# Unread TensorE products, early ACT table loads and moved weight products in a four-stage image network on one core

## The chip, the core and the metric

The kernel runs on one core of one Trainium2 chip. The core has a matrix engine (TensorE, called PE in the profile, with its weight loads listed apart as PEld), three engines for elementwise work (VectorE or DVE, ScalarE or ACT, GpSimd or POOL) and SyncE (SP), which here only starts transfers. In the kernel each engine has its own list of instructions, and the lists wait for one another by semaphores. Matrix products are written to tiles in PSUM; all other tiles are in SBUF.

The metric is the device time of one execution in microseconds. A kernel's time is the median of its runs.

## What is computed

The input x is one image of 256 by 256 positions with 32 channels, in 32-bit floats. Four layers follow one another, and each has the form "x plus something of the group norm of x":

```python
x = x + _L0_conv_ref(_gn(x), ...)   # layer norm over channels, gates and values, projection
x = x + _L1_conv_ref(_gn(x))        # 3x3 mean, Sobel gradients, their magnitude
x = x + _L2_conv_ref(_gn(x))        # the same again
x = x + _L3_conv_ref(_gn(x), ...)   # two-layer gated recurrence over 256 steps
```

`_gn` normalises over all positions and pairs of channels, so no layer can begin before the layer ahead has ended: the mean and the variance need the whole image. In layer 0 the sequence axis has length one, so its softmax is 1 and what remains is sigmoid(n Wg) * (n Wv), then a product with Wo. The recurrence has 256 sequences, two layers and 128 hidden units; each step makes four gates per layer from a product, normalises each gate's 128 values, and updates a cell and a hidden state.

## The kernel before

Everything is kept in two SBUF tiles, `xa` and `xb`, of 128 partitions (4 columns of the image by 32 channels) by 64 blocks by 256 rows. Blocks are taken in 32 pairs of 512 columns, and most instructions are 128x512. Where the code is written inside `tc.manual_schedule()`, the engines' orders are the orders of the code; elsewhere a scheduler may move instructions.

The stages, in order:

- **Input** (lines 163 to 185). `nat` is loaded in 16 transfers, PE transposes it (L176), ACT copies it to `xa` (L183), DVE takes `bn_stats` (L184). `group_norm` (L136 to L156) then turns the statistics into `scale` and `bias`: DVE `mv` (L139), PE `pm` (L141), DVE `mean`, `d`, `q` (L143 to L147), PE `pv` (L149), ACT `std` by a square root (L151), DVE `scale` and `bias` (L153, L155). The same function serves all four layers, so there are four such seams.
- **LayerNorm** (L201 to L264). PE centres each pair (`pc`, L238), ACT squares it, DVE keeps it in `xb`, PE sums the squares into `pvar` (L228). Then ACT takes the root `std` (L248), DVE its reciprocal `rstd` (L249), PE spreads it over the channels (`pb`, L254), DVE multiplies (L261) and POOL applies gamma and beta (L262). Two small constant tiles for this stage, `avg` and `spread`, are made by POOL (L205 to L211) in a pool that opens after the input stage.
- **Attention** (L268 to L332): products `pg` and `pv` (L279), a sigmoid on ACT (`sg`, L294), a multiply on DVE (`o`, L297), the projection (L303), `r` on ACT (L311), an add on POOL (L313), `bn_stats` (L316).
- **Two Sobel layers** (`sobel_layer`, L345 to L504). For each pair k, ACT normalises (`xp`, `xn`, L376), DVE makes `u`, part of `pp`, `v` (L383, L392, L397), POOL the differences `dh` and sums `sh` (L405, L401), PE the products `centre` (L412, L422) and `edges` (L452) into two PSUM tiles `pg0` and `pg1` of three buffers each, ACT squares (L458), DVE adds (`ss`, L462), ACT takes the root in place in `pg1` (L466), DVE adds the residual (L469) and takes statistics (L472). The order on all engines is a written list: each part has a due time within a period of `every = 4.0`, and the list is sorted by it. The first Sobel layer also runs, after each pair's statistics, one entry of the list `between`: the centring of the recurrence's weights (`centring`, L583).
- **Recurrence weights.** `products` (L607 to L626) runs between the two Sobel layers, in the seam of the third group norm: a transpose `pl`, ACT's copy `latt`, POOL's repeats `lat4` and `wout4`, two products `pf` added to `bc` by DVE, a product `pe` copied into `e4` by four ACT copies and completed by POOL. `finish` (L628 to L655) runs after the fourth group norm: `sb` from scale and bias, two products `pg` copied to `fx` by ACT (L642), `pk` (L644, L645), `cst4`.
- **Recurrence** (`recurrence`, L720 to L906): four units (layer l, half h of the sequences) per step, interleaved by the due times of `PLAN` with a period of 8.7; `project` (L763) starts a unit's `zz` from the input `xt`, L790 and L795 add the hidden states' products, `sq`, `ve`, `rs` normalise, ACT makes gates, DVE and POOL the cell, PE transposes `h` into `pt` (L853). Outputs of block `blk` end in `st` (L883) and four transfers on SP's queue (L885). `sums` and `roots` hold 64 steps of small results (`SLOTS`).

ACT's functions come from tables: a root and a sigmoid need different ones, and a load (ACT_TABLE_LOAD) stands ahead of the first function that needs the other.

Of the kernel before, what the change touches and what calls it, by code (L numbers as in the profile page):

```python
# [10 lines left out]
F32 = mybir.dt.float32  # L11
AF = mybir.ActivationFunctionType
ALU = mybir.AluOpType
# [45 lines left out]
def net_kernel(  # L59
# [71 lines left out]
    NST = NB // 2  # L131

# [3 lines left out]
    def group_norm(stats, psum):  # L136

        mv = small.tile([P, nc.vector.BN_AGGR_DIM], F32, name="mv")
        nc.vector.bn_aggr(mv, stats)  # L139
        pm = psum.tile([P, 1], F32, name="pm", tag="pm", bufs=1)  # L140
        nc.tensor.matmul(pm, lhsT=kt[:, K_GN, :], rhs=mv[:, 0:1], start=True, stop=True)  # L141
        mean = small.tile([P, 1], F32, name="mean")
# [6 lines left out]
        nc.tensor.matmul(pv, lhsT=kt[:, K_GN, :], rhs=q, start=True, stop=True)  # L149
        std = small.tile([P, 1], F32, name="std")  # L150
# [5 lines left out]
        return scale, bias  # L156

# [5 lines left out]
    with tc.tile_pool(name="nat", bufs=3) as natp, tc.tile_pool(  # L163
# [21 lines left out]
        gn = group_norm(stats, ps_in)  # L185
# [9 lines left out]
    KS = NST // 4  # L195
# [5 lines left out]
    with tc.tile_pool(name="ln", bufs=4) as lnp:  # L201


        avg = lnp.tile([P, KS, KS, J], F32, name="avg", bufs=1)
        nc.gpsimd.memset(avg, 0.0)  # L205
        for ks in range(KS):
            nc.gpsimd.tensor_copy(avg[:, ks, ks, :], kt[:, K_AVG, 0:P:C])
        spread = lnp.tile([P, KS * J, C], F32, name="spread", bufs=1)
        for g in range(4):
            rows = slice(g * C, (g + 1) * C)  # L210
            nc.gpsimd.tensor_copy(  # L211
                spread[rows], ident[rows, rows].unsqueeze(2).to_broadcast([C, KS * J, C])
            )
        rstd = lnp.tile([P, 2 * S], F32, name="rstd", bufs=1)
        with tc.tile_pool(name="ps_ln", bufs=6, space=PSUM) as ps_ln, tc.tile_pool(
# [32 lines left out]
            nc.scalar.activation(std, pvar, AF.Sqrt, bias=ln_eps)  # L248
            nc.vector.reciprocal(rstd, std)  # L249
        with tc.tile_pool(name="ps_sp", bufs=8, space=PSUM) as ps_sp:  # L250
            for k, g, ks in pairs:
# [10 lines left out]
                nc.gpsimd.tensor_scalar(  # L262
                    pair(xb, k), pair(xb, k), gamma4, beta4, ALU.mult, ALU.add
# [5 lines left out]
    with tc.tile_pool(name="at", bufs=3) as atp, tc.tile_pool(  # L269
# [48 lines left out]
        with tc.manual_schedule():  # L318
            together((), [(0, j) for j in range(J)])
            together((), [(1, j) for j in range(2)])  # L320
            for i in range(NST):
# [5 lines left out]
                if i >= 1:  # L327
                    project(i - 1)
            for i in range(NST - 1, NST):
                project(i)  # L330
# [4 lines left out]
    with tc.tile_pool(name="ps_gn", bufs=1, space=PSUM) as ps_gn:  # L335
        gn = group_norm(stats, ps_gn)
# [8 lines left out]
    def sobel_layer(src, dst, scale, bias, between):  # L345
# [152 lines left out]
        with tc.manual_schedule():  # L498
            for _, k, part, args in todo:
                part(k, *args)  # L500
                if part is statistics and between:
                    between.pop(0)()
# [4 lines left out]
    with tc.tile_pool(name="ps_n", bufs=1, space=PSUM) as ps_n:  # L507
        gn = group_norm(stats, ps_n)
        rw.products(ps_n)
    stats = sobel_layer(xb, xa, *gn, [])  # L510
# [8 lines left out]
    with tc.tile_pool(name="ps_n", bufs=1, space=PSUM) as ps_n:  # L519
        gn = group_norm(stats, ps_n)  # L520
        weights = rw.finish(lw, ps_n, gn)
    with tc.If(plain > 0) as arms:
# [28 lines left out]
class RecurrentWeights:  # L551
# [31 lines left out]
    def centring(self):  # L583
# [21 lines left out]
        return [lambda p=out[i : i + 2]: [f() for f in p] for i in range(0, len(out), 2)]  # L605

    def products(self, psum):  # L607
        nc = self.nc
        pl = psum.tile([P, KX], F32, name="pl")
        nc.tensor.transpose(pl, self.lat, self.ident[:KX, :KX])  # L610
        nc.scalar.copy(self.latt, pl)
        for dst, src in ((self.lat4, self.latt[:, 0:C]), (self.wout4, self.wout)):
            nc.gpsimd.tensor_copy(dst, src.unsqueeze(1).to_broadcast([P, J, C]))
        for l in range(L):
            pf = psum.tile([KX, G], F32, name="pf", bufs=2)
# [3 lines left out]
        pe = psum.tile([P, C], F32, name="pe")  # L619
        nc.tensor.matmul(  # L620
            pe, lhsT=self.lat4.rearrange("p j c -> p (j c)"), rhs=self.wout, start=True, stop=True
        )
        for j in range(J):
            rows = slice(j * C, (j + 1) * C)
# [323 lines left out]
```

## Time and profile before

| | us |
|---|---|
| runs of before | 2879.49, 2883.52, 2886.28 (median 2883.52) |
| the profiled execution | 2880.13 |
| its span, first to last instruction | 2878.2 |
| PE busy in the span | 2776.8 (96%) |
| DVE, ACT, POOL busy | 2401.1, 2369.6, 1722.2 |
| input, from 0 to the end of the last `bn_stats` | 34.2 |
| LayerNorm, from the first `pc` to the first `pg` | 41.0 to 105.7 |
| attention, to the last `bn_stats` | 105.7 to 329.2 |
| first Sobel layer, first `xp` to last `bn_stats` | 334.3 to 479.2 |
| second Sobel layer | 485.1 to 627.1 |
| recurrence, from the first `zz` | 636.3 to 2878.2 |

The profile is of one execution. Its page gives busy shares per engine, the span in 40 slices of 72 us, the chain of work that ended last, and groups of instructions by line. Queries of the trace give the same for any stretch: a timeline (start, duration, engine, line, operation, tile written and tiles read, and in brackets the engine's idle time before and who ended it), the chain in order of time, and windows (each engine's busy time and the granted clock of PE in each). The granted clock is 1.00 or 0.50 in the windows of this trace that hold no change of it. A wait for several semaphores is put down to the one that came last by the profile.

### The profile page before, as it was taken

What the parts mean: (1) busy time and instruction counts of PE and PEld (TensorE: products, weight loads), DVE (VectorE), ACT (ScalarE), POOL (GpSimd) and SP (SyncE); (2) the same over time, 40 slices, a digit from 0 to 9 for tenths busy, and PEclk for the clock granted to TensorE, in tenths of its full rate; (3) what the DMA queues carried; (4) which work ended last, traced back from release to release, by engine and by line L of the source; (5) the groups of instructions that cost most, each with busy time, mean ns of one, the idle gap of its engine ahead of it and who ended that gap; (6) DMA issues with size and microseconds to landing.
All of it is one profiled execution on the core that took longest, in us unless ns stands there. A gap on an engine that the chain in (4) does not pass through costs nothing.

```text
span 2878.2 us, 38258 instructions
## 1 busy us (share of the span) xinstructions
PE 2776.8 (96%) x9561; PEld 1034.1 (36%) x9561; DVE 2401.1 (83%) x6505; ACT 2369.6 (82%) x6961; POOL 1722.2 (60%) x2076
## 2 busy tenths in 40 slices
PE   7899898989999999999999999999999999999997
PEld 4433333333333333333333333333333333333332
DVE  6788797977888888888888888888888888888886
ACT  5477676758888888888888888888888888888886
POOL 2311374656666666666666666666666666666665
PEclk9899998989999999999999999999999999999999
DMA  3000000000000000000000000000000000000000
GB/s 133 1 1 1 16 1 1 1 22 8 12 12 12 13 13 12 12 12 11 12 12 12 12 12 12 12 13 15 12 14 13 13 12 12 13 12 12 5 4 9
DMA packets 94333, 38.37 MB, mean 13 GB/s; under 512 B 74852, under 2 KB 91269, under 8 KB 94104
## 3 DMA queue, kind: packets, MB, share of 16 engines
q1 hardware_dynamic: 93156, 34.67, 5.1%
q8 instruction: 81, 1.33, 0.2%
q14 instruction: 148, 1.21, 0.1%
q10 hardware_dynamic: 148, 0.86, 0.1%
q0 software_dynamic: 800, 0.30, 0.0%
HBM read 10.63 MB, written 8.39 MB: 7 GB/s over the span
## 4 chain that ended last, share of the span: by engine, by line
PE 76%; DVE 9%; POOL 7%; ACT 5%; issue 1%; DVEq 0%; POOLq 0%; ACTq 0%
PE zz L795 26%; PE zz L770 15%; PE zz L790 11%; PE pt L853 5%; POOL rs L811 4%; PE pv L279 4%; PE pg L452 4%; DVE c L841 4%; PE pg L412 3%; DVE ve L808 3%; ACT sq L803 3%; PE pg L303 2%; POOL fc L837 2%; ACT ga L784 1%; PE px L871 1%; PE pg L279 1%
## 5 line engine op out<-in xcount | busy, mean ns | idle before, releaser
L811 POOL TENSOR_TENSOR rs<-ve,mhalf 128x4 f32<-128x4 f32 x1024 | 1040.6, 1016 | 539.6 <-DVE ve L808 539.5
L795 PE MATMUL zz<-wc,hT 128*128 128x512 f32 x2040 | 1102.3, 622 | 0.0
L784 ACT ACTIVATE ga<-zz,rs 128x128 f32<-128x128 f32 x3072 | 986.5, 368 | 29.1 <-POOL rs L811 9.9
L808 DVE TENSOR_REDUCE ve<-sq 128x4 f32<-128x516 f32 x1024 | 703.0, 687 | 52.1 <-ACT sq L803 37.2
L803 ACT ACTIVATE sq<-zz 128x512 f32<-128x512 f32 x1024 | 610.2, 596 | 150.9 <-PE zz L795 142.7
L770 PE MATMUL zz<-fx,xt 33*128 33x512 f32 x2048 | 591.7, 643 | 0.8 <-ACT fx L642 0.8
L790 PE MATMUL zz<-wc,hT 128*128 128x512 f32 x1024 | 524.5, 594 | 0.0
L795 PEld LDWEIGHTS zz<-wc,hT 128*128 128x128 f32 x2040 | 324.5, 188 | 555.6 <-DVE hT L857 399.0
L832 DVE TENSOR_TENSOR c<-ga 128x128 f32<-128x128 f32 x1024 | 299.4, 292 | 167.4 <-ACT ga L784 72.3
L845 ACT ACTIVATE th<-c 128x128 f32<-128x128 f32 x1024 | 316.0, 309 | 100.8 <-DVE c L841 100.7
L848 DVE TENSOR_TENSOR h<-go,th 128x128 f32<-128x128 f32 x1024 | 309.5, 302 | 96.9 <-ACT th L845 96.9
L784 ACT ACTIVATE go<-zz,rs 128x128 f32<-128x128 f32 x1024 | 378.8, 370 | 0.0
L837 POOL TENSOR_TENSOR fc<-ga,c 128x128 f32<-128x128 f32 x510 | 232.2, 455 | 244.0 <-ACT ga L784 244.0
L841 DVE TENSOR_TENSOR c<-c,fc 128x128 f32<-128x128 f32 x1020 | 361.6, 355 | 18.4 <-DVE hT L857 0.5
L853 PEld LDWEIGHTS pt<-ident,h 128*128 128x128 f32 x1024 | 142.8, 139 | 542.8 <-DVE h L848 542.3
L853 PE MATMUL pt<-ident,h 128*128 128x128 f32 x1024 | 294.3, 287 | 36.3 <-DVE h L848 36.2
L857 DVE COPY hT<-pt 128x128 f32<-128x128 f32 x1024 | 293.2, 286 | 10.2 <-PE pt L853 2.7
L770 PEld LDWEIGHTS zz<-fx,xt 33*128 33x128 f32 x2048 | 162.2, 185 | 260.6 <-ACT ga L784 193.2
L862 POOL TENSOR_TENSOR hs<-hT,hT 128x256 f32<-128x256 f32 x256 | 198.1, 774 | 2.5 <-DVE hT L857 2.5
L297 DVE TENSOR_TENSOR o<-pv,sg 128x512 f32<-128x512 f32 x256 | 158.1, 681 | 45.8 <-PE pg L279 37.7
L790 PEld LDWEIGHTS zz<-wc,hT 128*128 128x128 f32 x1024 | 162.4, 198 | 68.2 <-issue 56.4
L294 ACT ACTIVATE sg<-pg 128x512 f32<-128x512 f32 x256 | 138.6, 599 | 31.0 <-PE pg L279 25.0
(140 smaller groups left out, 2313.4 us busy)
## 6 DMA issues: line engine op xcount, KB each, us to landing
xt<-xa SPq DMA_DIRECT2D x256, 64.0 KB, 2.0
nat<-in_x_dram SPq DMA_DIRECT2D x16, 512.0 KB, 6.7
out_dram<-st SPq DMA_DIRECT2D x256, 32.0 KB, 1.7
wc<-in_L_conv_W_cell_dram SPq DMA_DIRECT2D x2, 512.0 KB, 4.6
kt<-in_consts_dram ACTq DMA_DIRECT2D x1, 832.0 KB, 5.8
wv<-in_L_conv_Wv_dram POOLq DMA_DIRECT2D x4, 32.0 KB, 4.1
wg<-in_L_conv_Wg_dram POOLq DMA_DIRECT2D x4, 32.0 KB, 5.5
gamma<-in_L_conv_ln_gamma_dram POOLq DMA_DIRECT2D x4, 0.1 KB, 5.9
```

The costliest lines, as they stand in the source:

```text
L770: nc.tensor.matmul(zz, lhsT=x, rhs=fx[rows, l, :], start=True, stop=l == 0 and t == 0)
L784: nc.scalar.activation(dst, gates(x, g), func, scale=scale)
L790: nc.tensor.matmul(get("zz"), lhsT=v["hT", 0, t][:, seqs], rhs=wc[:, l, 0, :], start=False, stop=t == 0)
L795: nc.tensor.matmul(get("zz"), lhsT=v["hT", l, t - 1][:, seqs], rhs=wc[:, l, 1, :], start=False, stop=True,)
L803: nc.scalar.activation(sqs[l, h][:, :, 0:H], four(get("zz")), AF.Square, scale=float(H**-0.5))
L808: nc.vector.tensor_reduce(ve, sqs[l, h], AX.X, ALU.add)
L811: nc.gpsimd.tensor_tensor(rs, get("ve"), inputs.mhalf, ALU.pow)
L832: nc.vector.tensor_mul(c, gates(get("ga"), 0), gates(get("ga"), 3))
L841: nc.vector.tensor_add(c, c, get("fc"))
L845: nc.scalar.activation(th, get("c"), AF.Tanh)
L848: nc.vector.tensor_mul(hh, get("go"), get("th"))
L853: nc.tensor.transpose(pt[:, 0:P], get("h"), ident)
```

## The change

Five things are changed.

1. `busy(psum, n, rhs)` issues n products of the identity with 256 columns into a PSUM tile `junk` that nothing reads. `group_norm` calls it before `pm` (3, 7, 3 and 3 products in the four seams), between `pm` and `pv` (2) and after `pv` (2, 12, 12 and 3). Nine more such products go into `pvar` after `std` of the LayerNorm, four follow the last `pb`, and the recurrence has six after its first two `zz` products and two after the next one.
2. `table(func, after)` issues a one-column activation that nothing reads. With Sqrt it follows the last input copy, and stands before the last projection's `r` of attention; with Sigmoid it follows the LayerNorm's `std`, and the fourth group norm's `scale`. The load of that table goes with it.
3. `avg` and `spread` are made at the start of the kernel in the constants' pool. Of the gamma/beta operations, every second one is ACT's instead of POOL's. `SLOTS` is 32 instead of 64.
4. `products` no longer runs between the Sobel layers. It returns five pieces that run after the statistics of pairs 0 to 4 of the second Sobel layer, with their PSUM tiles from the three buffers of `pg1`. In `finish`, the second `fx` copy is DVE's. The memsets of ones in `xt` are written after `finish`; in POOL's order they keep their place.
5. Of the last block's four output transfers, two are issued by ACT.

```diff
+    def table(func, after):
+        t = small.tile([P, 1], F32, name="table")
+        nc.scalar.activation(t, after, func, scale=0.0, bias=one)
+
+    def busy(psum, n, rhs=None):
+        junk = psum.tile([P, S], F32, name="junk", tag="junk", bufs=1)
+        for _ in range(n):
+            nc.tensor.matmul(
+                junk, lhsT=ident, rhs=kt[:, 0:2, :] if rhs is None else rhs, start=True, stop=True
+            )
...
-    def group_norm(stats, psum):
+    def group_norm(stats, psum, before, after, rhs=None):
...
         nc.vector.bn_aggr(mv, stats)
+        busy(psum, before, rhs)
         pm = psum.tile([P, 1], F32, name="pm", tag="pm", bufs=1)
         nc.tensor.matmul(pm, lhsT=kt[:, K_GN, :], rhs=mv[:, 0:1], start=True, stop=True)
+        busy(psum, 2, rhs)
...
         nc.tensor.matmul(pv, lhsT=kt[:, K_GN, :], rhs=q, start=True, stop=True)
+        busy(psum, after, rhs)
         std = small.tile([P, 1], F32, name="std")
...
-        gn = group_norm(stats, ps_in)
+        table(AF.Sqrt, xa[:, NB - 1, 0:1])
+        gn = group_norm(stats, ps_in, 3, 2, xa[:, NB - 1, :])
...
             nc.scalar.activation(std, pvar, AF.Sqrt, bias=ln_eps)
+            table(AF.Sigmoid, std[:, 0:1])
             nc.vector.reciprocal(rstd, std)
+            for _ in range(9):
+                nc.tensor.matmul(
+                    pvar[:, 0:S], lhsT=ident, rhs=kt[:, 0:2, :], start=True, stop=True
+                )
...
                 nc.vector.tensor_mul(pair(xb, k), pair(xb, k), pb)
-                nc.gpsimd.tensor_scalar(
-                    pair(xb, k), pair(xb, k), gamma4, beta4, ALU.mult, ALU.add
-                )
+                if i % 2:
+                    nc.scalar.activation(
+                        pair(xb, k), pair(xb, k), AF.Identity, scale=gamma4, bias=beta4
+                    )
+                else:
+                    nc.gpsimd.tensor_scalar(
+                        pair(xb, k), pair(xb, k), gamma4, beta4, ALU.mult, ALU.add
+                    )
+            junk = ps_sp.tile([P, 2 * S], F32, name="pb")
+            for _ in range(4):
+                nc.tensor.matmul(
+                    junk[:, 0:S], lhsT=ident, rhs=kt[:, 0:2, :], start=True, stop=True
+                )
...
+            table(AF.Sqrt, one)
             for i in range(NST - 1, NST):
                 project(i)
...
-        gn = group_norm(stats, ps_gn)
+        gn = group_norm(stats, ps_gn, 7, 12)
...
                 if part is statistics and between:
-                    between.pop(0)()
+                    between.pop(0)(lambda: flat(ps_s.tile([P, 2, S], F32, name="pg1")))
...
-        gn = group_norm(stats, ps_n)
-        rw.products(ps_n)
-    stats = sobel_layer(xb, xa, *gn, [])
+        gn = group_norm(stats, ps_n, 3, 12)
+    stats = sobel_layer(xb, xa, *gn, rw.products())
...
-        gn = group_norm(stats, ps_n)
+        gn = group_norm(stats, ps_n, 3, 3)
+        table(AF.Sigmoid, gn[0])
         weights = rw.finish(lw, ps_n, gn)
+        inputs.ones()
...
+        return [
+            turn,
+            repeat,
+            lambda ps: biases(ps, 0),
+            lambda ps: biases(ps, 1),
+            output,
+        ]
...
-            nc.scalar.copy(fx[0 : X1 + KX, l, :], pg)
+            copy = nc.vector.tensor_copy if l else nc.scalar.copy
+            copy(fx[0 : X1 + KX, l, :], pg)
...
-SLOTS = 64
+SLOTS = 32
...
-                nc.sync.dma_start(
+                queue = nc.scalar if blk == NB - 1 and j % 2 else nc.sync
+                queue.dma_start(
...
+    at(-1e4, busy, 6)
     at(PLAN[1, 1]["x"] - PERIOD, project, 0, 0, 1)
+    at(PLAN[1, 1]["x"] - PERIOD, busy, 2)
```

## The prediction

> **What bounds the kernel now.** I read the page's slices first, then the chain of waits, then the timeline around each pause of PE, and last windows of PE cut at the clock's own step. The page's clock row:
>
> ```profile
> PEclk9899998989999999999999999999999999999999
> ```
>
> The granted clock is below full only in slices 0, 5, 7 and 9 of 40: the seams between stages. From 653 us to 2865 us (77% of the span) it is full, and the instruction orders of before and after agree row for row there, so I leave the recurrence's steady part at its time. All that can move is the first 653 us and the tail.
>
> The clock changes at 83.04, 89.87, 96.70 and 113.77: steps of 2, 2 and 5 times 3.413 us. I cut PE's span on that grid (columns: window, length, PE busy, clock):
>
> ```profile
> core 0: us, PE busy (x), PEclk, DMA share, GB/s
> 339.05:342.46 3.41, 3.39 (x8) 0.50 0.00 0
> 342.46:345.87 3.41, 3.41 (x12) 1.00 0.00 0
> ...
> 475.58:478.99 3.41, 0.24 (x2) 1.00 0.00 0
> 478.99:482.41 3.42, 3.33 (x6) 0.50 0.00 0
> ...
> 622.35:625.77 3.42, 1.09 (x5) 1.00 0.24 58
> 625.77:629.18 3.41, 0.55 (x2) 0.50 0.40 96
> ...
> 646.25:649.66 3.41, 3.41 (x8) 0.50 0.00 0
> ```
>
> The clock seems decided at a window's end by the work in it. A window with 0.24 or 1.09 us of work lost the clock; one with 1.74 us (2861.50 to 2864.91) kept it, so the limit lies between. One full of 128x256 products (339.05) brought it back, and these have the shape of the change's unread products. Windows full of products with 33 rows or columns (all of 478.99, a third of 646.25) did not.
>
> What such a seam costs, from the timeline:
>
> ```profile
> 38.38 1.28 ACT L151 ACT_TABLE_LOAD   x1 [5.26 <-PE pv L149]
> ...
> 86.37 19.22 DVE L261 TENSOR_TENSOR xb<-xb,pb 128x512 f32<-128x512 f32 x32 [2.16 <-PE pb L254]
> ...
> 107.82 1.28 ACT L294 ACT_TABLE_LOAD   x1 [26.99 <-PE pg L279]
> ...
> 345.24 0.69 DVE L462 TENSOR_TENSOR ss<-sq,pg 128x512 f32<-128x512 f32 x1 [1.98 <-ACT sq L458]
> ...
> 497.41 0.69 DVE L462 TENSOR_TENSOR ss<-sq,pg 128x512 f32<-128x512 f32 x1 [3.56 <-ACT sq L458]
> ```
>
> Three table loads stand on the path: these two and one at 332.31. A fourth, at 639.08, does not (E). The two L462 rows are the first `ss` of each Sobel layer: before them DVE waits, and after them its waits list, bar one of 0.72 us at the next `u`, is empty until the layer's last pairs. Each layer is then a fixed DVE run of some 4.13 us a pair, and a seam is worth what it moves the first `ss`.
>
> **The change part by part.** One unread product (128x256) takes 0.48 us at full clock and 0.91 at half: the L422 groups of four took 1.92 us (471.82) and 3.64 us (339.07). Times below are those of before.
>
> A. Input to LayerNorm. The Sqrt load now follows the last copy (33.12) and is done by 34.7, before `pv` ends: -1.28. POOL's `spread` and `avg` copies ran at 32.3 to 37.64 and held up DVE's `d` and `q` (0.47 and 1.05 us, where the second group norm has 0.16 and 0.22): 1.14 us gone, since they now run at about 19 us, in POOL's idle 13 us. There they lie beside bn_stats, whose pace stayed 0.62 us when the first copies ran beside it at 32.3, so nothing; without that cover the 1.14 at most comes back. Two products between `pm` and `pv` end at 36.8, `q` at 36.46: +0.3; two after `pv` +0.3. The dense stretch 40.98 to 45.48 at half clock is 4.5 us, so 2.25 if the clock holds. Three products from 33.2 leave each window some 1.4 us or more: near the limit. Ends: held -1.8 - 2.25 = -4.1; lost, the pairs cost 1.2 and 1.1 and it is -0.1. I take -3.0, nearer held, as products bring the clock back sooner anyway.
>
> B. LayerNorm to attention. Nine products (4.3 us from 80.9) end at 85.2, `rstd` at 84.22: `pb` is 1.0 later, but its first four take about 1.05 instead of 2.1: nothing. The pause before them is 0.85 us, so no clock is lost. Half of POOL's gamma/beta work goes to ACT. The chain puts 18 us on it:
>
> ```profile
> 87.27 18.03 POOL xb L262 x24
> 105.30 0.40 issue
> 105.70 2.14 PE pg L279 x8
> ```
>
> but I don't believe it: DVE's 32nd multiply ends at 86.37 + 19.22 = 105.59, PE starts 0.1 later, and the banks of `pg` are those that DVE then frees. DVE's 0.60 a pair stays, so this part is worth nothing (ACT's 0.80 per pair fits into 1.2). Should POOL have been the releaser, the four products still hold PE to the same time. They start when `pb` ends (102.9), at half clock, and end at 106.5: +0.8. The Sigmoid load goes beside the reciprocal: -1.28. From 109.3 the clock should be back (dense since 102.9) where it came at 113.77: 4 us at half are -2.0. Sum -2.5; ends -4.3 (clock never lost) and -0.4 (no gain in clock).
>
> C. Attention to Sobel 1. The load now stands before the last `r`, which waits 0.45 for it: -0.83. Seven products start when that `r` frees the banks (327.6) and end at 331.0: +0.2; two before `pv` +0.3; `xp` comes 0.4 earlier. Twelve products end at 338.95, with `dh` at 338.6. `centre` then takes 1.92 instead of 3.64, POOL has lost a `wout` copy of 0.75, and the first `ss` comes at about 343.2: -2.0. PE's pause is 1.4 us, so I take the clock as held. Ends -2.6 and +2.4 (lost, and twelve products ahead of `centre`).
>
> D. Sobel 1 to 2. Chain of waits:
>
> ```profile
> 475.64 2.95 issue
> 478.58 0.23 PE pl L610
> ```
>
> PE sits still for 2.95 us, and in the rows behind these two `pf` products take 1.92 and 1.85 us, one ahead of `pm` and one ahead of `pv`. They go; `xp` can start at 483.3 instead of 485.05. Held, the twelve products end at 488.4 and `ss` comes at 493.0: -4.4. But PE pauses from 475.61 to 478.58, and the 622.35 row says the clock is likelier lost: then three and two products at 0.91 move `pv` to 484.1, and the twelve end between 490.4 (clock back at once) and 492.4: `ss` -2.5 to -0.5; I take -2.5. In layer 2 DVE pays for two `bc` adds, 0.62 each, in a run with no slack: +1.25. The products take `pg1` buffers, three in all; PE's `centre` of pair k+2 starts 1.2 to 1.9 us before pair k's residual ends, and with a buffer taken it must wait for it: 0 to 1.5, I take 0.8. Sum -0.45; ends -3.15 and +2.75.
>
> E. Sobel 2 to recurrence. The load at 639.08 lies beside `ve` and `rs` (ACT waited 0.78 more): nothing. Held: `zz` at 634.65 instead of 636.33, its first product 1.0 shorter, then `zz` and `hT` products 2.1 shorter less 0.96 for two unread ones, and the next 1.05: -4.9 at the third transpose `pt` (654.20). Lost (pause 623.45 to 626.38) and back by 633: `zz` at 636.3, the rest -3.0. Lost and not back, since `pg` and `zz` have 33 rows: `zz` +3.2, six products in front of the first transpose, +2.9 in all. I take -3.0. The `ones` memsets keep their place in POOL's order, and SLOTS adds no wait.
>
> F. Tail. The last block's four issues take 0.635 each on SP (5.08 for 8); two go to ACT, idle then: -1.25, ends -1.3 and 0.
>
> Sum -3.0 - 2.5 - 2.0 - 0.45 - 3.0 - 1.25 = **-12.2**. The profiled execution took 2880.1 us (span 2878.2 and 1.9 around it): 2867.9. The median shown is 3.4 above that execution: **2871**.
>
> Two rules of the Trainium skill. "TensorE: Matmul & The Clock Gate", in "Why this matters for your kernels", has the clock fall only after pauses of about 3 us or more; D's and E's (2.97 and 2.93) would pass and all seams be held, 2863; here the clock fell 2.3 us after PE's last product (623.45 to 625.77). "ScalarE: Activation LUTs", "What ACT_TABLE_LOAD costs", adds a drain of 1.38 to 1.28 us; three loads would be 8.0, not 3.84, and the sum 4.1 better; here the next ACTIVATE starts 0.01 us after the load.
>
> **The rivals.**
> Held everywhere: -4.1 - 4.3 - 2.6 - 3.15 - 4.9 - 1.3 = -20.3, 2863. For: most products come within 3 us; against: the 622.35 row.
> No change: the clock is lost in A, D and E and comes back late, and the buffers stall: -0.1 - 1.0 - 2.0 + 2.25 + 2.9 - 1.25, about +1: 2884. For: the dense but cold window 646.25.
> Slower: unread products run at half clock to their last one, in front of the work that PE is waited for. Twelve take 10.9 us: `centre` is 5 late in C and D, with D's 2.05 on top; in E `zz` is 3.2 late, six products add 2.0 and two more 1.8: +7. With the rest, -0.1 - 0.4 + 5 + 7 + 7 - 1.25 = +17: 2900. It decides once a dense stretch of these products stays cold for more than two windows; the 339.05 row speaks against it.
>
> **How the numbers follow.** Forecast 0.58, held everywhere 0.20, no change 0.17, slower 0.05. The range leaves out the slower rival, half of no change and some of held: 2861 to 2884. Counting by 0.2% (5.8 us, about what a measurement of this kernel tells from none): faster 0.78 (forecast and held), same 0.16, slower 0.06.
>
> **What would show it.** From the last `stats` of the stage before to the first `ss` it is now 16.75 us (328.49 to 345.24) and 18.9 (478.52 to 497.41): these should fall to about 14.3 and 16.4. No table load should stand between `pv` and `std`, and `d` and `q` of the first group norm should take 0.16 and 0.22. The `pg` after attention's first four should come 2 us or so after them, not 4. Layer 2 should be about 2 us longer from first to last `ss`, and the third transpose of the recurrence some 3 us nearer to the last `stats`. The clock should be full but for `pb`'s DVE-paced stretch and short pieces in D and E. A clock at half through the twelve products would make me wrong, as would a recurrence that isn't the same.

## Result and the profile after

The changed kernel takes 2868.53 us (median of 5 runs, 2866.43 to 2868.9) beside 2882.91 us for the kernel before in the same session: ratio 0.9949, 95% interval 0.9934 to 0.9964. It is faster by half a per cent. The forecast was 2871 us within 2861 to 2884. The profiled execution took 2867.98 us, its span is 2866.2 us (2878.2 before).

The page's clock row of the changed kernel has one slice left below full:

```profile
PEclk9899999999999999999999999999999999999999
```

That slice holds `pb`. The losses in Sobel 2's seam and at the start of the recurrence are too short for a slice; they show in windows cut on the clock's own steps (window, length, PE busy, clock):

```profile
core 0: us, PE busy (x), PEclk, DMA share, GB/s
464.50:467.91 3.41, 1.76 (x8) 1.00 0.00 0
467.91:471.33 3.42, 2.05 (x5) 0.50 0.00 0
471.33:474.74 3.41, 3.41 (x11) 0.50 0.00 0
474.74:478.15 3.41, 3.41 (x17) 1.00 0.00 0
...
614.68:618.10 3.42, 1.10 (x5) 1.00 0.49 110
618.10:621.51 3.41, 3.41 (x11) 0.50 0.38 84
621.51:624.92 3.41, 3.41 (x7) 0.50 0.43 98
624.92:628.34 3.42, 2.91 (x10) 1.00 0.46 104
628.34:631.75 3.41, 3.41 (x6) 0.50 0.31 70
...
641.99:645.41 3.42, 1.83 (x7) 1.00 0.00 0
```

A window decides the clock of the next one. 1.10 us of work in 614.68 to 618.10 lost it, as 1.09 did before. But 1.76 us in 464.50 to 467.91 lost it too, and 2.91 us in 624.92 to 628.34. The first is all `edges` on 64 rows; the second is mostly `pg` and `zz` on 33 rows. Busy time alone is not what is counted; what is counted stands at the end of the part on why the prediction was right.

The timeline of the changed kernel, for the steps that the prediction named (start, busy time, engine, line, operation):

```profile
33.74 1.28 ACT L137 ACT_TABLE_LOAD   x1
...
36.41 0.16 DVE L161 TENSOR_TENSOR d<-mv,mean 128x1 f32<-128x1 f32 x1
36.61 0.22 DVE L163 SCALAR_TENSOR_TENSOR q<-d,mv 128x1 f32<-128x1 f32 x1
...
76.18 1.28 ACT L137 ACT_TABLE_LOAD   x1
81.59 19.22 DVE L285 TENSOR_TENSOR xb<-xb,pb 128x512 f32<-128x512 f32 x32 [2.04 <-PE pb L278]
...
335.55 0.69 DVE L497 TENSOR_TENSOR ss<-sq,pg 128x512 f32<-128x512 f32 x1 [1.24 <-ACT sq L493]
485.22 0.69 DVE L497 TENSOR_TENSOR ss<-sq,pg 128x512 f32<-128x512 f32 x1 [1.24 <-ACT sq L493]
489.67 1.10 PE L447 MATMUL pg<-dh,kt 128*128 128x512 f32 x2 [1.16 <-DVE xa L504]
499.20 0.66 DVE L658 TENSOR_TENSOR bc<-bc,pg 33x512 f32<-33x512 f32 x1
614.40 11.02 POOL L741 MEMSET xt<- 1x2048 f32 x6
622.01 1.61 DVE L689 TENSOR_SCALAR sb<-ident,scale 32x32 f32<-32x32 f32 x1
```

The first two loads are off the path, `d` and `q` are as short as forecast, DVE's 32 multiplies are as long as before, and the two first `ss` come 9.69 and 12.19 us earlier (345.24 and 497.41 before). Against it stand a wait of 1.16 us of PE in layer 2, two `bc` adds on DVE, and one thing that the prediction did not see: the small `sb` writes took up to 1.61 us where they took 0.57 before. The timeline of the kernel before:

```profile
623.88 11.02 POOL L680 MEMSET xt<- 1x2048 f32 x6
...
630.70 0.57 DVE L634 TENSOR_SCALAR sb<-ident,scale 32x32 f32<-32x32 f32 x1
```

There too the write ends with a memset, the fourth (623.88 + 4 x 1.84 = 631.2, and 630.70 + 0.57 = 631.3). It only started closer to that end.

The two profiled executions by stage, from the starts of these rows; the stage times of all kernels follow below:

| stage | predicted | measured |
|---|---|---|
| last input `bn_stats` (the input came later) | 0 | +0.53 |
| A: first `bn_aggr` to LayerNorm `std` | -3.0 | -5.19 |
| B: `std` to second `bn_aggr` | -2.5 | -2.36 |
| C: second `bn_aggr` to first `ss` | -2.0 | -2.67 |
| layer 1 | 0 | +0.34 |
| D: seam -2.84 and layer 2 +2.72 | -0.45 | -0.12 |
| E: fourth `bn_aggr` to the first output block's `fin` (to the third `pt`, where the forecast placed it: -0.83) | -3.0 | -0.19 |
| rest of the recurrence, to the last `fin` | 0 | -1.87 |
| F: last `fin` to the end | -1.25 | -0.46 |
| sum | -12.2 | -12.0 |

The sum is right partly because errors cancel: A gave 2.2 more than taken, E 2.8 less, and the recurrence 1.9 that were in no term.

### The profile page after: what moved, and what is told of

The parts are those of the page before. It is cut to its first block, busy times and chain, and to the rows that moved or that the text cites. A ratio compares the mean times of both kernels' runs of the same rounds, so it can differ in the third digit from the quotient of the medians.

```text
span 2866.2 us, 38549 instructions
## 1 busy us (share of the span) xinstructions
PE 2796.5 (98%) x9709; PEld 1056.9 (37%) x9709; DVE 2400.1 (84%) x6506; ACT 2379.1 (83%) x6980; POOL 1710.6 (60%) x2061
## 3 DMA queue, kind: packets, MB, share of 16 engines
q8 instruction: 82, 1.34, 0.2%
## 4 chain that ended last, share of the span: by engine, by line
PE 59%; DVE 7%; POOL 6%; ACT 4%; issue 1%; ACTq 0%; POOLq 0%; DVEq 0%
PE zz L853 26%; PE zz L828 15%; PE zz L848 12%; PE pt L911 5%; POOL rs L869 4%; DVE c L899 4%; DVE ve L866 3%; ACT sq L861 3%; POOL fc L895 2%; PE px L934 1%; ACT ga L842 1%; PE px L931 1%; DVE h L906 1%; PE px L925 0%; POOL hs L920 0%
```

## Experiments

Theory: the gain is the clock kept or returned by unread products (6 to 9 us), three table loads (3.8) and POOL's copies out of DVE's way (1.1), less what layer 2 pays. Rivals: the products are worth nothing; POOL's share of gamma and beta is what held attention; the loads lengthen pauses and act by the clock. All edits are to the changed kernel unless said otherwise. Not undone by itself in any run: `SLOTS` (64 or 32) and the second `fx` copy in `finish`; their shares in the recurrence and in E are open.

Stage times in us from each profile. A, B, C, D (the seam) are as above; L2 is first `ss` to last `bn_aggr` of layer 2; E is that `bn_aggr` to the recurrence's third `pt`; R is from there to the end. The ratio is to the kernel before, run in the same session.

| kernel | A | B | C | D | L2 | E | R | median | ratio (95%) |
|---|---|---|---|---|---|---|---|---|---|
| before | 45.95 | 249.08 | 16.02 | 18.16 | 129.67 | 27.12 | 2224.0 | 2882.91 | 1 |
| changed | 40.76 | 246.72 | 13.35 | 15.32 | 132.39 | 26.29 | 2222.3 | 2868.53 | 0.9949 (0.9934-0.9964) |
| e1 | 43.20 | 248.37 | 15.73 | 15.93 | 132.39 | 27.26 | 2222.8 | 2876.38 | 0.9981 (0.9971-0.9990) |
| e2 | 42.16 | 250.81 | 14.63 | 14.47 | 132.40 | 25.50 | 2223.6 | 2872.47 | 0.9965 (0.9951-0.9979) |
| e3 | 40.75 | 246.07 | 13.59 | 17.01 | 129.65 | 24.54 | 2221.3 | 2865.76 | 0.9946 (0.9932-0.9959) |
| e4 | 43.40 | 246.12 | 13.35 | 15.54 | 132.39 | 25.50 | 2223.9 | 2869.81 | 0.9958 (0.9944-0.9972) |
| e5 | 40.75 | 246.69 | 13.34 | 13.23 | 132.39 | 22.72 | 2222.2 | 2861.91 | 0.9929 (0.9915-0.9943) |
| e6 | 40.75 | 245.99 | 13.35 | 13.23 | 132.39 | 23.33 | 2221.8 | 2862.63 | 0.9931 (0.9917-0.9945) |
| e7 | 40.75 | 248.96 | 13.34 | 14.48 | 130.16 | 25.55 | 2225.4 | 2865.24 | 0.9941 (0.9926-0.9955) |
| e8 | 40.75 | 246.57 | 13.35 | 13.22 | 130.15 | 23.42 | 2224.7 | 2861.64 | 0.9930 (0.9916-0.9944) |
| e9 | 40.75 | 258.26 | 13.35 | 13.22 | 132.36 | 23.67 | 2222.6 | 2874.81 | 0.9968 (0.9956-0.9980) |
| e10 | 40.75 | 256.62 | 13.34 | 13.22 | 130.12 | 23.40 | 2227.8 | 2872.92 | 0.9963 (0.9950-0.9977) |
| e11 | 40.75 | 248.13 | 13.35 | 13.22 | 132.39 | 22.72 | 2222.4 | 2865.92 | 0.9939 (0.9925-0.9952) |
| e12 | 40.75 | 246.54 | 13.35 | 13.23 | 130.16 | 23.68 | 2225.6 | 2865.22 | 0.9935 (0.9922-0.9949) |

**e1: no unread product.**

```diff
-        busy(psum, before, rhs)
...
-        busy(psum, 2, rhs)
...
-        busy(psum, after, rhs)
...
-            for _ in range(9):
...
-            for _ in range(4):
...
-    at(-1e4, busy, 6)
-    at(PLAN[1, 1]["x"] - PERIOD, busy, 2)
```

> All unread products are left out (three group norms, nine after the LayerNorm, four before attention, six and two in the recurrence); the rest of the change stays. Theory (the prediction's): they are worth what they do to the clock. Against the changed kernel's stage times: last input bn_stats to LayerNorm std 40.8 becomes about 43 (clock half until some 45 us); LayerNorm std to the last r of attention 241.8 becomes 243 to 244; last stats to first ss 14.07 becomes 15.5 to 16 in Sobel 1, and 16.05 becomes 17 to 18 in Sobel 2; last stats to the third pt of the recurrence 27.0 becomes 28 to 30. In all +7 to +10: 2876 to 2879. Rival (the gain is that of the table loads, POOL's copies and the moved weight products; unread products are worth nothing): each of these intervals within 0.4 of the changed kernel's, 2868 to 2870.

Measured: ratio 0.9981 against 0.9949. By the table A is 2.44 longer, B 1.65, C 2.38, D 0.61 and E 0.97: 8.1 us. The rival falls: the products that nobody reads carry more than half of the gain, and they do it by the clock, which without them is half for 18 steps of 3.41 us in A, C, D and E together and with them for 7. In D they are worth less than forecast, in E the low end of it.

**e2: no table load ahead.** The four calls of `table` are removed.

```diff
-        table(AF.Sqrt, xa[:, NB - 1, 0:1])
...
-            table(AF.Sigmoid, std[:, 0:1])
...
-            table(AF.Sqrt, one)
...
-        table(AF.Sigmoid, gn[0])
```

> The four one-column ACTIVATEs that load a table ahead are left out; everything else of the change stays. Theory: three of the loads come back on the path, 1.28 in the LayerNorm's seam, 1.28 before attention's first sg, 0.83 in Sobel 1's seam, and the fourth costs nothing: +3.4, 2872; last input bn_stats to LayerNorm std 40.8 becomes 42.1, last stats to first ss of Sobel 1 14.07 becomes 14.9, last stats to third pt of the recurrence stays 27.0 within 0.4. Rival (the loads lengthen PE's pauses so that the clock is lost with them): 44 or more in the first interval, 16 or more in Sobel 1, in all +7: 2875. Rival (the unread products alone carry the gain, a load is hidden by them): within 0.5 of the changed kernel, 2868.5.

Measured: A +1.40, `std` to first `sg` +1.23 (28.03 to 29.26), C +1.28: three loads of 1.28, and nothing besides them in the stages where they stand. The attention after the first `sg` was 2.86 longer, for the clock fell there for two steps. The first, from 108.3, follows PE's wait for the late `sg` (0.28 us of work from 106 to 108): there the first rival has a point, a load in a seam can cost the clock as well. The second, from 320.0, is the loss that e7 shows below without any edit near. D and E were 0.85 and 0.79 shorter, by fewer or later steps at half clock. The second rival (a load is hidden) falls. The fourth load costs nothing, as forecast.

**e3: weight products back in the seam.** Part 4 undone, `products` as before.

```diff
-        gn = group_norm(stats, ps_n, 3, 12)
-    stats = sobel_layer(xb, xa, *gn, rw.products())
+        gn = group_norm(stats, ps_n, 3, 12)
+        rw.products(ps_n)
+    stats = sobel_layer(xb, xa, *gn, [])
```

> Part 4 is undone: the weight products go back into the seam before Sobel 2, beside the unread products, and layer 2 has none. Theory: the seam is longer by the two 33-column bias products, 1.9 us each at half clock, partly covered by the unread ones (last stats to first ss 16.05 becomes 18 to 20), and layer 2 is shorter by what it paid (first ss to last stats 131.66 becomes 128.9 to 129.1); the two about cancel, 2867.5 to 2870. Rival (the products in the layer cost more than the seam gained): 16.05 becomes less than 17.5, and the time is 2866 to 2867.

Measured: the seam is 1.69 longer and the layer 2.74 shorter. The expected seam (18 to 20 from the last `stats`) was too long: it is 17.7, the clock was half for one step of 3.41 and not for two. At these clocks part 4 costs about 1 us where it stands. E was 1.75 shorter with two steps at half clock instead of five, and nothing of the edit lies there. The rival has the time about right (2865.76), but not the seam of less than 17.5; in whole runs the two versions can't be told apart (0.9946 and 0.9949).

**e4: three small parts undone at once.** Gamma and beta all on POOL, `avg` and `spread` copied inside the LayerNorm, last transfers on SP alone.

```diff
-    avg = cp.tile([P, KS, KS, J], F32, name="avg")
...
+        avg = lnp.tile([P, KS, KS, J], F32, name="avg", bufs=1)
...
-                if i % 2:
-                    nc.scalar.activation(
...
-                queue = nc.scalar if blk == NB - 1 and j % 2 else nc.sync
-                queue.dma_start(
+                nc.sync.dma_start(
```

> Three small parts are undone at once, each read in its own stage: gamma and beta of the LayerNorm all on POOL again, the avg and spread copies on POOL inside the LayerNorm again, and the last block's output transfers all on SP again. Theory: gamma and beta are worth nothing, since DVE's multiplies set the first pg (LayerNorm std to first pg 26.5 stays within 0.2); POOL's copies again hold up DVE's d and q (1.05 to 1.14 more in last input bn_stats to std: 40.8 becomes 41.9); the transfers cost 1.25 at the end by the prediction, 0.3 to 0.5 by the changed kernel's trace (last o0 to the end of the span 13.4 becomes 13.7 to 14.7). In all +1.4 to +2.4, 2870 to 2871. Rival (POOL's 32 passes release attention): the first pg comes 3 to 5 us later and the time is 2874 to 2876.

The timeline of e4 in A and B:

```profile
34.98 3.21 POOL L227 COPY spread<-ident 32x1024 f32<-32x1024 f32 x3
36.44 0.67 DVE L161 TENSOR_TENSOR d<-mv,mean 128x1 f32<-128x1 f32 x1
37.15 1.05 DVE L163 SCALAR_TENSOR_TENSOR q<-d,mv 128x1 f32<-128x1 f32 x1
...
85.15 23.99 POOL L283 TENSOR_SCALAR xb<-xb,gamma,beta 128x512 f32<-128x512 f32 x32 [46.96 <-DVE xb L282]
...
104.37 1.14 PE L305 MATMUL pg<-xb,wg 32*128 32x512 f32 x8
```

POOL passes over gamma and beta until 109.14, and attention's `pg` start at 104.37, 26.22 after `std`; in the changed kernel it is 26.49. The chain of waits that put 18 us on POOL named the wrong engine: the split to ACT is worth nothing. `d` and `q` are 1.34 longer together. But A is 2.64 longer: PE waited 1.07 for `q`, the step from 35.60 to 39.01 held 2.11 us of work, and the next was half, with the first `pc` in it. The copies cost twice, once on DVE and once by the clock, and the prediction had priced only the first.

**e5: unread products in the pause itself.**

```diff
                 if part is statistics and between:
...
+                if part is edges and k == NST - 1 and args == (0,):
+                    junk = flat(ps_s.tile([P, 2, S], F32, name="pg0"))
+                    for _ in range(6):
+                        nc.tensor.matmul(
+                            junk[:, 0:S], lhsT=ident, rhs=kt[:, 0:2, :], start=True, stop=True
+                        )
```

> The changed kernel with six more unread products at the end of each Sobel layer, in a free pg0 buffer, right behind the last edges: in the changed kernel PE sits still there for 3.02 us, and the clock falls. Theory: that pause is what loses the clock in Sobel 2's seam and in the recurrence's start, so it is now full through both; the changed kernel lost it for 6.8 us in the one and for three pieces in the other. Last bn_aggr to first ss of Sobel 2 15.32 becomes 13.6 to 14.3; last bn_aggr to third pt of the recurrence 26.3 becomes 23 to 24.5; in all -2.5 to -4.5: 2864 to 2866. Rival (the clock goes by the work in a window of 3.4 us, and the gap from the last product to the statistics' pm still leaves one short): both intervals within 0.7 of the changed kernel's, 2868.

The timeline of e5 at the end of layer 2, and then its windows:

```profile
611.46 2.86 PE L541 MATMUL pg<-kt,ident 128*128 128x256 f32 x12
614.55 1.53 PE L143 MATMUL junk<-kt,ident 128*128 128x256 f32 x6 [0.24 <-DVE xa L504]
...
618.32 1.03 DVE L695 TENSOR_SCALAR sb<-ident,scale 32x32 f32<-32x32 f32 x1
...
622.43 1.95 PE L834 MATMUL zz<-fx,xt 33*128 33x512 f32 x4 [0.51 <-DVE e L716]
```

```profile
core 0: us, PE busy (x), PEclk, DMA share, GB/s
614.31:617.73 3.42, 3.02 (x16) 1.00 0.45 102
617.73:621.14 3.41, 3.20 (x10) 1.00 0.42 96
621.14:624.55 3.41, 2.90 (x10) 1.00 0.45 104
624.55:627.97 3.42, 3.42 (x9) 0.50 0.39 91
```

The changed kernel's own three products start only when DVE's last residual has freed the banks, 3.02 us after PE's last product; these six do not wait for it. The pause is 0.24, the clock is full through D and nearly all of E, D falls to 13.23 and E to 22.72: 5.7 us, more than expected. The one step still lost follows the window 621.14 to 624.55, 2.90 us of work without a pause over 0.51, some 2.1 of it on 33 rows and most of the rest in one-column products. This version beats the kernel before, and its five runs (2860.62 to 2863.06) all lie below the changed kernel's five, though the intervals of the two ratios, from two sessions, just overlap.

**e6: e5 with the memsets of ones cut in four.**

```diff
-                self.nc.gpsimd.memset(xt[p + C : p + KX], 1.0)
+                row = xt[p + C : p + KX].rearrange("p k j s -> p (k j s)")
+                for i in range(4):
+                    self.nc.gpsimd.memset(row[:, i * 512 : (i + 1) * 512], 1.0)
```

> e5 with each of the six one-partition memsets of ones on POOL (1.84 each) cut into four of 512 elements. Theory: DVE's small sb writes wait for the end of the POOL memset that is running, since in five kernels their end falls within 0.04 of such a boundary; with pieces of some 0.46 they wait at most that long: the first sb write 1.6 becomes 0.6 to 0.9, and the recurrence's pg and all behind it 0.7 to 1.1 earlier against e5. Rival (sb is slow for another reason, the table load of ACT beside it or the pieces cost POOL as much): sb stays at 1.6, and the third pt where e5 has it.

The timeline of e6:

```profile
611.89 11.67 POOL L749 MEMSET xt<- 1x512 f32 x24
618.25 0.48 DVE L695 TENSOR_SCALAR sb<-ident,scale 32x32 f32<-32x32 f32 x1
```

The first `sb` takes 0.48 instead of 1.03, while POOL's memsets still cover it: DVE waits for the end of the POOL instruction that runs, not for all of them. (In the changed kernel the fifth memset ends at 614.40 + 5 x 1.84 = 623.6, and the `sb` of 622.01 at 623.62.) The mechanism holds; the gain does not: `zz` came 0.28 earlier, bounded by the products ahead of `pg`, and two steps of half clock instead of one took back 0.9 behind it. Whole runs: 0.9931 beside 0.9929.

**e7: cheaper weight products in layer 2.**

```diff
-                    between.pop(0)(lambda: flat(ps_s.tile([P, 2, S], F32, name="pg1")))
+                    between.pop(0)(lambda: flat(ps_s.tile([P, 2, S], F32, name="pg0")))
...
-            nc.vector.tensor_add(self.bc[:, l, :], self.bc[:, l, :], pf)
+            nc.scalar.copy(self.fx[0:KX, l, :], pf)
+            nc.gpsimd.tensor_add(self.bc[:, l, :], self.bc[:, l, :], self.fx[0:KX, l, :])
```

> The changed kernel with the weight products inside Sobel 2 made cheaper for DVE and PE: their buffers are those of pg0, which ACT frees, instead of pg1, which DVE's residual frees, and each bias product goes by an ACT copy and an add on POOL instead of an add on DVE. Theory: first ss to last bn_aggr 132.39 is 129.65 without the products, and DVE's two adds (1.25), PE's wait for the residual (1.2) and two waits of u for ACT make the difference; it becomes 129.9 to 130.6, in all -1.8 to -2.5: 2866 to 2867. Rival (the adds on POOL hold up DVE as its copies did in the LayerNorm, and ACT's copies come in front of xn): 131.2 or more, 2867.5 to 2869.

Measured: L2 is 130.16, as expected, and PE waits for no residual in the layer any more. D is 0.84 shorter (one step of half clock instead of two), while B is 2.24 longer. 1.65 of that stand at attention's end, in the timeline and the windows of e7:

```profile
313.04 4.11 PE L313 MATMUL pv<-xb,wv 32*128 32x512 f32 x12
317.07 5.09 PE L337 MATMUL pg<-o,wo 128*32 128x512 f32 x32
```

```profile
core 0: us, PE busy (x), PEclk, DMA share, GB/s
313.22:316.63 3.41, 3.41 (x12) 1.00 0.00 0
316.63:320.05 3.42, 3.42 (x17) 0.50 0.00 0
```

The same place in the changed kernel:

```profile
311.34 3.91 PE L313 MATMUL pv<-xb,wv 32*128 32x512 f32 x12
315.18 3.64 PE L337 MATMUL pg<-o,wo 128*32 128x512 f32 x32
```

```profile
core 0: us, PE busy (x), PEclk, DMA share, GB/s
310.91:314.33 3.42, 3.42 (x19) 1.00 0.02 5
```

Six `pv` on 32 rows, 4.1 us without a pause, fill one step of the clock, and the next is half: the projection's products (`pg` from `o` and `wo`) take 5.09 instead of 3.64. The same six stand in the changed kernel, from 311.34 to 315.25, and there the clock stays. Nothing differs but where the steps fall: there the step also takes in products that ran side by side just ahead of the six.

**e8: e5, e6 and e7 together.**

> e5, e6 and e7 together. Theory: they lie in different stages and add up: -5 to -8 against the changed kernel, 2861 to 2863.5. Rival (what one stage gains, the start of the recurrence or the clock's phase gives back): 2865 to 2868.

The stages add up (D 13.22, L2 130.15), yet the time is e5's: 0.9930 beside 0.9929. E is 0.7 longer by two steps of half clock, and R is 2.5 longer. R is 2224.7 to 2227.8 in the four kernels with e7's edit and 2221.3 to 2223.9 in the other eight and the changed one. Part of it is two slips of 0.5 us at output blocks 10 and 18, which the kernel before has at the same two places. What makes them I can't say; the instruction orders of the recurrence are the same.

**e9 and e10: the clock held through `pb`.** One unread product ahead of every second `pb`, and eight instead of four behind the last; e10 has e8 under it.

```diff
                 pb = ps_sp.tile([P, 2 * S], F32, name="pb")
+                if i % 2:
+                    nc.tensor.matmul(
+                        pb[:, 0:S], lhsT=ident, rhs=kt[:, 0:2, :], start=True, stop=True
+                    )
```

> e5 with one unread product ahead of every second pb of the LayerNorm's spread, written into the pb buffer that the real product then overwrites, and eight unread products instead of four behind the 32nd. Theory: what loses the clock there is not a pause, since PE is busy all the time, but that a product with 32 rows of input counts little; 0.48 us of a 128-row product in every 1.2 us (DVE takes 0.60 a pair, PE then some 1.0 of 1.2) is about 1.4 in each 3.4 us, near the limit, and should keep it full: LayerNorm std to first sg 28.0 becomes 26.2 to 26.6, the rest of attention 0 to 0.5 shorter, DVE's 32 multiplies still 19.2; in all -1.4 to -2.2 against e5, 2860. Rival (a busy PE in this stretch is cold for another reason, or 1.4 us a window is too little): the clock falls as before, PE at half then takes 2.0 per two pairs where DVE takes 1.2, DVE's multiplies stretch to 27 or more, and the first sg is 6 or more later: 2868.

> e8 with e9's products in the LayerNorm's spread. Theory: -1.4 to -2.2 against e8: 2859.5 to 2860.5. Rival (as for e9): 2868.

The timeline of e9:

```profile
81.41 0.70 PE L279 MATMUL pb<-kt,ident 128*128 128x256 f32 x2
82.04 1.13 PE L282 MATMUL pb<-rstd,spread 32*128 32x512 f32 x4
83.10 0.70 PE L279 MATMUL pb<-kt,ident 128*128 128x256 f32 x2
```

Theory and rival are both wrong about the time, and the theory is right about the clock: it is full through `pb` and nearly all of attention, so a 128-row product of 0.5 us and two `pb` in every 1.7 hold it. But PE takes 1.69 for two `pb` and a product, DVE's multiplies wait, and the first `sg` is 10 us later. I had priced a `pb` at a quarter of 1.05.

**e11 and e12: products ahead of every fourth `pb`.** Two of them, and six behind the last; e12 has e7's edit as well, with whole memsets.

```diff
+                for _ in range(2 if i % 4 == 0 else 0):
+                    nc.tensor.matmul(
+                        pb[:, 0:S], lhsT=ident, rhs=kt[:, 0:2, :], start=True, stop=True
+                    )
```

> e5 with two unread products ahead of every fourth pb (not one ahead of every second) and six behind the 32nd instead of four. e9 held the clock, but PE then took 1.69 for two pb and a product (0.53 for a pb at full clock, 0.63 for the product), more than DVE's 1.20. Theory: consecutive pb use different groups of 32 rows and run side by side, and a 128-row product between them ends that; with four pb in a row PE takes about 1.05 for them and 1.0 to 1.2 for the products, under DVE's 2.40. The clock stays full, DVE's multiplies take 19.2 to 19.6, LayerNorm std to first sg 28.0 becomes 26.2 to 27.0; -1 to -2 against e5, 2860 to 2861. Rival (a pb costs PE 0.53 at full clock whatever stands beside it): 3.2 for four pb and two products against 2.4, eight times: the first sg comes 6 or 7 later, 2868.

> e11 with e7's cheaper products in Sobel 2 (pg0 buffers, ACT copies and POOL adds); the memsets stay whole. Theory: first ss to last bn_aggr of Sobel 2 130.15 as in e7 and e8, instead of 132.39, and the recurrence starts that much earlier: 2.2 less than e11, 2858 to 2859. Rival (in e8 the recurrence's own stretch was longer by about what layer 2 had gained): within 0.7 of e11.

The timeline of e11:

```profile
81.79 1.13 PE L279 MATMUL pb<-kt,ident 128*128 128x256 f32 x4
82.85 1.14 PE L282 MATMUL pb<-rstd,spread 32*128 32x512 f32 x8
...
84.01 19.22 DVE L289 TENSOR_TENSOR xb<-xb,pb 128x512 f32<-128x512 f32 x32 [3.10 <-PE pb L282]
```

Four `pb` in a row take 1.14, two took 1.13: four different groups of 32 rows run side by side, and a 128-row product between them ends that. The clock is full and DVE's run is 19.22 again. The gain is still nothing (`std` to first `sg` 27.84 beside 28.00): the two products ahead of the first `pb` start DVE 1.06 later, about what the four cold products behind the last had cost (0.93 at the first `pg`, by e1). In whole runs, taken in two sessions, the ratios of e11 and e5 (0.9939 and 0.9929) can't be told apart. Its profile is 3.3 us longer: 1.67 because the input ended later, 1.6 because the clock fell once at attention's end, as in e7. Layer 2 in e12 is 130.16 again, and R 2225.6: again the gain does not reach the end.

## Why the prediction was right, step by step

The time was forecast within 2.5 us and the causes are those it named. That the sum (-12.2) meets the two profiled executions (-12.1) so closely is luck: by the medians the gain is 14.4, the runs of the kernel before spread over 6.8 us, and terms that were off cancel. Step by step:

- **A**, taken as -3.0, was -5.2, beyond its end "held" of -4.1. The three terms were right: the load 1.28 (e2: 1.40), the contention 1.14 (e4: 1.34), the clock 2.25 (e1: 2.44). The two 0.3 for unread products did not show: at full clock `pm`, `pv` and `pcb` were shorter, and the products stood in waits. The clock was held in A in all eleven profiles that have the products and the early copies, wherever the steps fell; in e4 a wait of 1.07 was enough to lose it.
- **B**, -2.5, was -2.4. Its terms hold: the load 1.23 (e2), the products ahead of attention 0.93 at the first `pg` where 0.8 was taken (e1), and the clock 2.0 behind the first `sg` (e1). That POOL's half of gamma and beta is worth nothing, against the chain of waits, is shown by e4.
- **C**, -2.0, was -2.7: the load was worth 1.28 and not 0.83, and the clock was held.
- **D**: the seam, taken as -2.5 with the clock lost, was -2.84 with the clock lost. Layer 2 was +2.72 and not +2.05: DVE's two adds were as priced, PE's longest wait for a buffer was 1.16, within what was taken, and two waits of DVE's `u` for ACT, 0.69 and 0.45, were left out. D's upper end, put on record as +2.75, is +2.25 by its own terms (-0.5, 1.25 and 1.5).
- **E** is the step that failed. Taken was a clock lost in the pause and back by 633, `zz` no later than before, and -3.0 at the third `pt`. Measured are `zz` 0.64 later (9.89 behind the last `bn_aggr`, 9.25 before), -0.83 at the third `pt` and -0.19 at the first output block. The three products in front of `pm` started only after the pause of 3.02 us, so the clock was half from 618.10 to 624.93. Two things were not in the prediction: DVE's `sb` waited 1.0 us longer for a POOL memset that it had called harmless, "keep their place in POOL's order"; and the clock fell again twice, behind a step of mostly 33-row products (624.92) and behind one with a wait of 1.59 in it (641.99). e5 shows what the pause was worth: E 3.6 shorter, 4.4 below the kernel before, where the end "held" was -4.9.
- "I leave the recurrence's steady part at its time" was wrong by 1.9: 1.0 of it are the two slips that only the kernel before has of the two, and 0.4 is output block 52, which is 0.4 shorter in the changed kernel and in most others. What makes either is open. It hid E's failure.
- **F**, -1.25, was -0.46. From the last `st` to the end it is 7.46 in the kernel before and 8.61 in e4, with all issues on SP, and 6.63 to 7.65 in the eleven kernels and the changed one with two queues: some gain, within a scatter as large as itself.

The rivals. "Held everywhere" would have been right for D's seam and for E had the products stood in the pause; e5 is that kernel. Its 2862 beside the 2863 worked out is partly luck: in e5 `pb` still loses the clock (B -2.4, not -4.3) and A gave 1.1 more. "Slower" needed twelve cold products; they were cold for no more than one step.

The two rules. The clock rule of "TensorE: Matmul & The Clock Gate" ("Why this matters for your kernels": pauses of about 3 us and more) does not describe these runs. The changed kernel's pauses in D and E are 3.02 us, but the clock fell 1.66 us into the one (466.26 to 467.92) and 1.10 us after the other had ended (617.00 to 618.10), each time at the end of a step; in e4 it fell behind a step with no wait over 1.07, in e5 behind one of mostly 33-row products with none over 0.51, and in e7 behind a step that 32-row products filled. The same page ("What's actually happening") has the window 3413 ns long and free-running; the steps here are 3.41, and their position was worth 1.6 us in attention. The drain of 1.38 per load of "ScalarE: Activation LUTs" is not seen: three loads brought 1.40, 1.23 and 1.28. "SBUF — State Buffer" ("SBUF: two separate sides") has a port pair that GpSimd and certain DVE operations take in turn, each for a whole instruction; `sb` and the memsets in e6 agree.

What a step is counted by can be read from the traces. Give each matmul record (a product here leaves two, a transpose one) its columns times its rows / 128, and a quarter of that to products of 128 rows into 32 columns, which run four at a time (32 records of 512 columns in 3.64 us); add this up by steps, from 14 us on. In the 14 profiles, the 76 steps at full clock that lost it hold at most 1524, and the 11,431 that kept it at least 1560. Of the steps at half clock, the 62 that brought it back hold at least 1557, and the 116 that did not at most 1527, but for one of 1579. The limit stands between, about 1540; an unread product counts 512, so it takes about three of them a step. It explains the odd cases: 1.76 us of `edges` is 1418, e4's 2.11 us with one-column products 1416, e5's 2.90 us 689, the six `pv` 1375 in e7 and, with what the step takes in ahead of them, 1874 in the changed kernel, and a step of `pb` at DVE's pace 1443. The prediction's limit, between 1.09 and 1.74 us of busy time, was of the wrong quantity. The count was found in these traces afterwards; no run was made to test it.

## What to carry to other kernels

To keep the clock, an unread product must stand inside the pause, in a buffer that is free before the engine's wait ends; behind a pause of 3 us it came too late to keep the clock and only brought it back sooner (two steps at half instead of five in the seam of Sobel 2). Count the steps of the clock by columns times rows and not by busy time: products of 32 or 33 rows that run one after another stay near or under the limit, however dense, and a full-row product between 32-row ones costs their running side by side. Before a short DVE operation on the path, look for a long POOL instruction beside it, and read a gain of 2 us as luck until the steps of the clock have been laid over both traces.

## What was not expected of the hardware

- The clock goes by rows as well as by time: 2.9 us of mostly 33-row products in a 3.41 us window lost it (e5), 4.1 us of 32-row products lost it or not with the position of the steps (e7 and the changed kernel), and two 128-row products ahead of every four of 32 rows held it (e11). Columns times rows in a step separate nearly all 11,685 steps, at about three unread products.
- A 32x32 DVE write took up to 1.75 us (e7), to the end of a one-partition POOL memset of 1.84 us; with memsets of 0.49 it took 0.48 (e6).
- From the third `pt` to the end, with the same orders of instructions behind it, thirteen profiles took from 2221.3 to 2227.8 us; the slips of 0.5 us at fixed blocks are open.
